# Polynomial work of a fused convolution and attention kernel in two units of three rounds instead of three of two

## The chip, the core and the metric

The kernel runs on one core of a Trainium2 chip. The metric is the time of one execution on the device in microseconds (us), the median of three runs. The traces come from one further execution, taken by the hardware profiler.

## What is computed

The input `x` is 32 images of 64 channels and 56 x 56 positions. Two layers follow each other. Cut to what matters:

```
# layer 0: in each of 8 groups of 8 channels, all products of two and of three channels
p2 = x[:, :, I2] * x[:, :, J2]                    # 36 products
p3 = x[:, :, I3] * x[:, :, J3] * x[:, :, K3]      # 120 products
l  = x + (p2 . W2 + b2) * beta2 + 0.1 * (p3 . W3 + b3) * beta3
# layer 1: for each image, over its N = 56 * 56 = 3136 positions
g   = clip(bn1(conv1x1(l, w_inside)), 0, 6)
f   = theta^T theta                               # theta: the first 32 channels of l
f   = softmax(softmax(f, axis=1), axis=2)
out = bn2(depthwise3x3(g . f)) + l
```

The score matrix `f` is 3136 x 3136 for each image; it is made, normalised twice and used in strips and is never stored.

## The kernel before

**Pairs, steps and halves.** Images go in 16 pairs (`NP`), the two images of a pair on partitions 0 to 63 and 64 to 127. A pair takes `IT` = 49 steps: 24 strips of 128 query positions for its first image, one strip that both share (step 24, `kind == 2`), and 24 for its second. Every step makes 128 x 3136 scores. A step has two halves of 1568 scores. Half `h` counts halves from the start of a pair, so step `t` holds halves `2t` and `2t + 1`.

**One step `t`** (the loop at the end, lines 889 to 931) issues, in this order on TensorE: the scores of the first half (`scores(t, 0)`, into the four banks of the tile `ps`), the attention matmuls of the step three earlier (`attend(u, ...)` with `u = t - LAG`, `LAG` = 3) up to block `split(t)`, then whatever was put at `aux0`; then the scores of the second half, the rest of the attention blocks, and whatever was put at `aux1`. VectorE evicts each half of the scores from `ps` into the tile `e`, keeping the minimum of the negated scores (lines 553 to 561). ScalarE makes two passes over `e`: the exponential with its sum (`first_softmax(t)`), and, for the step before, the exponential of the normalised values (`second_softmax(t - 1)`). The tile `ps` has one buffer, `e` has four.

**Attention** is summed over the strips in PSUM: 25 blocks of 2 x 64 positions by 65 columns, 21 of them in the banks `av0` to `av2`, the last four in the first 260 columns (`AUX`) of the bank `ax`. At an image's end `take` (line 605) divides these sums out of PSUM on VectorE: for the second image of a pair parts 0 and 1 after step 2 of the next pair, parts 2 and 3 in its step 3; for the first image in step 27. Step 27 attends the shared strip for both images.

**The other columns of `ax`** (252) serve two kinds of small work, one after another, called units:

- *Polynomial units.* The layer 0 output of the next pair is made in 13 chunks (`NPC`) of 242 positions. A chunk has six rounds; in a round four matmuls (one for each image and half of its channels) add products of channels to `ax`. The products are made by GpSimd (`products`, line 362; 4 of the first round, `q`, then 4 in each of four rounds and one in the last, `p`) from copies of `x` that SP loads (`prefetch`). GpSimd may be ahead by 8 `q` and 20 `p` tiles (`ROOM`). After the sixth round VectorE adds bias and `x` and writes `y` (`poly_out`, line 469).
- *g units.* The 1 x 1 convolution of three strips (`g_in`, six small matmuls; the ninth unit of an image has one), and its clipping into `gq` by VectorE (`g_out`).

Between units VectorE refills the columns of `ax` with zeros or with the bias (`prepare`, line 443).

**The schedule of the units** is written out for each pair `n` (lines 803 to 854). Each unit gets a half; an even half means `aux0`, an odd one `aux1`, so always behind that half's attention matmuls. For pairs 1 to 14 the three units of a chunk, with two rounds each, go to successive even halves; `BETWEEN` says how many g units follow after which chunk (first the current pair's second image, then the next pair's first), and they take the next free halves. Pair 0 and pair 15 have rules of their own. `split` (line 702) chooses how many attention blocks come before the second half's scores: a unit weighs `1 + 3.6 * rounds` blocks, a g unit 4, and the blocks are shared so that the two halves of a step weigh the same, between 7 and 17.

**Depthwise convolution.** 45 taps a pair on VectorE (`conv_step`) are spread over halves in which no unit ends (`leaves`, line 874).

**Order.** Every instruction is pinned behind the one before it on its engine (`pin`, line 89), so the order of issue above is the order of execution. Line 108 is the helper through which all instructions pass, and so the profile's rows all say L108: they are told apart by tile.

Of the kernel before, what the change touches and what calls it, by code (L numbers as in the profile page):

```python
# [24 lines left out]
NQ = N // QT  # L25
# [44 lines left out]
def tile_poly_conv_attention(  # L70
# [362 lines left out]
    def feed(n, c, ks):  # L433
        todo = [("x0" if name == "0" else "xs", name, k) for k in ks for name in "0a"]
        for name in "24bc":
            todo += [("xc", name, None)] if name == "c" else [("xs", name, k) for k in ks]
        for tag, name, k in todo:
            plan.append((tag, (n, c, ks, name, k)))
        feeds.append((products(n, c, ks), None))
# [78 lines left out]
    def tile_at(t):  # L518
        n, r = divmod(t, IT)
        return n, (0 if r < NQ else 2 if r == NQ else 1), r % (NQ + 1)  # L520
# [103 lines left out]
    def turn(b, h):  # L624

        if h == 0:
            tr = rp.tile([128, 2, NBL * QR], FP, name=f"tr_{b}", tag="tr")
            nums[b] = nums[b], tr
        num, tr = nums[b]
        dve.transpose(tr[:, h, :], num[:, h, :, :].rearrange("p i c -> p (i c)"))  # L630

    def place(b, h):

        _, tr = nums[b]
        o0 = (b % 2) * C + h * 32
        for j in range(2):
            blocks = N // QB - NBL if j else NBL
            for r in range(2):
                k = 2 * j + r
                dst = tt[o0 : o0 + 32, j * NBL * QB : (j * NBL + blocks) * QB]  # L640
                start(
                    dst.rearrange("p (i r q) -> p i r q", r=2, q=QR)[:, :, r, :],
                    tr[k * 32 : k * 32 + 32, h, : blocks * QR].rearrange("p (i q) -> p i q", q=QR),
                )
        if h == 1:
            del nums[b]
# [32 lines left out]
    def put(t, at, what):  # L679
        beside.setdefault((t, at), []).append(what)  # L680
# [5 lines left out]
    LAG = 3  # L686
    ALL, ONE, TWO = (0, 1, 2, 3), (0, 1), (2, 3)
# [32 lines left out]
    def poly_unit(n, c, ks, rs, hs):  # L720
        ends = rs[-1] == NRND
        unit(
            hs,
            FOR_POLY,
            lambda: poly(n, c, ks, rs),
            (lambda: poly_out(n, c, ks)) if ends else None,
            1 + 3.6 * len(rs),
        )
        if ends and c == NPC - 1:
            for j in (0, 1):  # L730
                if 2 * j in ks:

                    t = hs // 2 + 1 if j == 0 or n == 0 else (n * IT) + 2
                    put(t, "loads", lambda j=j: load_theta(2 * n + j))

    def g_unit(n, qs, j, hs):
        unit(hs, FOR_G, lambda: g_in(n, qs, j), lambda: g_out(n, qs, j), 4)
# [3 lines left out]
    def ready(qs):  # L741

        end = min(N, (qs[-1] + 1) * QT)
        return next(c for c, (p, w) in enumerate(PCS) if p + w >= end)
# [55 lines left out]

    BETWEEN = {0: 1, 1: 3, 2: 1, 3: 3, 4: 1}, {7: 1, 8: 1, 9: 1, 10: 3, 11: 1, 12: 2}
    for n in range(NP):
        base = n * IT
        gb = [("g", n, qs, 1) for qs in GS]
        ga = [("g", n + 1, qs, 0) for qs in GS]

        def rounds(m, c, ks, per):
            return [("p", m, c, ks, list(range(r, r + per))) for r in range(0, NRND + 1, per)]  # L810

        todo = []
        if n == 0:
            for c in range(NPC):
                todo += rounds(0, c, TWO, 3)
            todo += gb
            for c in range(NPC):
                todo += rounds(1, c, ALL, 2)
                if c >= NPC // 2 + 1:
                    k = min(2 if c < NPC - 1 else len(ga), sum(ready(g[2]) <= c for g in ga))  # L820
                    todo += ga[:k]
                    ga = ga[k:]
            free = [h for h in range(2, 2 * IT - 5) if h // 2 != NQ + LAG]
            at = [2 * base + free[i * (len(free) - 1) // (len(todo) - 1)] for i in range(len(todo))]
        elif n + 1 == NP:
            todo = gb
            at = [2 * (base + LAG) + 3 + 4 * i for i in range(len(gb))]
        else:
            at = []
            h = 2  # L830
            for c in range(NPC):
                for what in rounds(n + 1, c, ALL, 2):
                    h += h % 2
                    while h in (2 * LAG, 2 * (NQ + LAG)):
                        h += 2
                    todo.append(what)
                    at.append(2 * base + h)
                    h += 1
                for of, between in zip((gb, ga), BETWEEN):
                    for _ in range(between.get(c, 0)):  # L840
                        assert of is gb or ready(of[0][2]) <= c
                        while h in (2 * LAG, 2 * (NQ + LAG), 2 * (NQ + LAG) + 1):
                            h += 1
                        todo.append(of.pop(0))
                        at.append(2 * base + h)
                        h += 1
            assert not gb and not ga and h <= 2 * IT
        for what, hs in zip(todo, at):
            if what[0] == "p":
                poly_unit(*what[1:], hs)  # L850
            else:
                assert what[3] == 1 and hs >= 2 * (base + LAG) or hs > 2 * (base + NQ + LAG) + 1
                assert what[3] == 0 or hs < 2 * (base + NQ + LAG)
                g_unit(*what[1:], hs)
        if n + 1 < NP:
            put(
                max(base - 8, 1), "feed",
                lambda n=n: [feed(n + 1, c, ALL) for c in range(NPC)],
            )
        for b, end in ((2 * n, base + NQ), (2 * n + 1, base + IT - 1)):  # L860
            t = end + LAG
            for h in range(2):
                leaves.add(2 * (t + 2 + h))
                put(t + 2 + h, "gap0", lambda b=b, h=h: turn(b, h))

                put(t + 3 + h if b % 2 else base + IT + h, "loads", lambda b=b, h=h: place(b, h))
# [22 lines left out]
    while t < last + LAG or beside:  # L889
# [3 lines left out]
        if old:  # L893
            n, kind, q = tile_at(u)
# [111 lines left out]
```

## Time and profile before

| | |
|---|---|
| median of three runs | 4962.83 us (4959.59 to 4973.32) |
| the profiled execution's own time | 4963.24 us |
| its span, first to last instruction | 4961.4 us |
| mean granted TensorE clock | 0.988 |
| ScalarE, first exponential `e<-e,nm` | 784 of 2913 ns mean |
| ScalarE, second exponential `e<-e,rz` | 784 of 2896 ns mean |
| VectorE, eviction of a first half `e<-ps` | 784 of 1790 ns mean |
| VectorE, eviction of a second half `e<-ps,nm` | 784 of 1847 ns mean |
| GpSimd, products `p<-q,x`, `p<-q,xb`, `q<-x,xa` | 786, 740 and 732 ns mean |

A row of a timeline gives the start and the duration of an instruction, or of a run of like instructions, in us; then engine, line, operation, destination and source tiles, shape and number; in brackets how long the engine was idle before it and what it waited for. Each matmul of the program appears as two records (`x16` for the eight score matmuls of a half). Matmuls are pipelined, and the end of one is modelled: the distance between starts says more than the durations. A row of waits gives who waited for whom, the total in us, the number of waits and the longest.

### The profile page before, as it was taken

How to read it: one execution, taken by the hardware profiler on the slowest of the kernel's cores; microseconds unless marked ns; L12 is line 12 of the kernel's file. 1: busy time of each engine (PE TensorE's matmuls, PEld its weight loads, DVE VectorE, ACT ScalarE, POOL GpSimd, SP SyncE). 2: the span in 40 equal slices, each digit the busy share in tenths (PEclk: the TensorE clock that was granted, in tenths of full speed). 3: DMA queues.
4: the chain of work that ended last, by engine and by line, in shares of the span. 5: the costliest groups of instructions: out<-in, count | busy, mean ns of one | idle time of the engine just before them, and what ended most of it. 6: DMA issues, size and time to landing. Idle time of an engine off the chain costs nothing.

```text
span 4961.4 us, 263901 instructions
## 1 busy us (share of the span) xinstructions
PE 4711.5 (95%) x118068; PEld 3211.9 (65%) x118068; DVE 4136.2 (83%) x6106; ACT 4554.6 (92%) x2356; POOL 3212.2 (65%) x4325
## 2 busy tenths in 40 slices
PE   6988999999999999999999999999999999999885
PEld 2555666666666666666666666666666666666663
DVE  6545898988888898898988888888888888888787
ACT  1767999999999999999999999999999999999995
POOL 2676685857758586785857678585876858587000
PEclk9999999999999999999999999999999999999997
DMA  7555656565565556556565555656555565654101
GB/s 203 148 154 150 147 143 154 144 149 143 146 148 147 139 150 149 139 143 150 146 146 148 147 142 144 145 152 145 144 150 144 145 145 146 153 142 117 39 8 33
DMA packets 884029, 685.64 MB, mean 138 GB/s; under 512 B 290892, under 2 KB 868428, under 8 KB 878796
## 3 DMA queue, kind: packets, MB, share of 16 engines
q1 hardware_dynamic: 874892, 659.46, 52.1%
q8 instruction: 923, 15.12, 1.3%
q10 hardware_dynamic: 8000, 9.30, 0.6%
q14 instruction: 214, 1.75, 0.1%
HBM read 565.65 MB, written 25.69 MB: 119 GB/s over the span
## 4 chain that ended last, share of the span: by engine, by line
PE 76%; DVE 12%; DMA 3%; issue 3%; ACT 3%; POOL 1%; SPq 1%; ACTq 0%; POOLq 0%; DVEq 0%
PE av L108 33%; PE ps L108 25%; PE ax L108 18%; DVE e L108 10%; ACT e L108 3%; DMA xc_None<-in_x_dram 2%; DVE y L108 1%; SPq L108 1%; POOL p L108 1%; DVE num L108 1%; DMA x<-in_x_dram 1%; DMA first<-in_x_dram 1%; POOL q L108 0%; DMA xa<-in_x_dram 0%; ACTq L108 0%
## 5 line engine op out<-in xcount | busy, mean ns | idle before, releaser
L108 PEld LDWEIGHTS av<-gq,e 128*64 128x64 f32 x64512 | 2015.8, 138 | 945.6 <-issue 938.6
L108 ACT ACTIVATE e<-e,nm 128x3136 f32<-128x3136 f32 x784 | 2283.6, 2913 | 279.9 <-DVE e L108 264.0
L108 POOL TENSOR_TENSOR p<-q,x 128x242 f32<-128x242 f32 (+1 forms) x2418 | 1820.2, 786 | 842.6 <-PE ax L108 834.8
L108 ACT ACTIVATE e<-e,rz 128x3136 f32<-128x3136 f32 x784 | 2270.5, 2896 | 0.0
L108 PE MATMUL av<-gq,e 128*64 128x65 f32 x64512 | 2229.3, 225 | 4.3 <-ACT e L108 3.0
L108 DVE TENSOR_SCALAR_CACHE_REDUCE e<-ps 128x1568 f32<-128x1568 f32 x784 | 1403.4, 1790 | 312.7 <-PE ps L108 295.4
L108 DVE TENSOR_SCALAR_CACHE_REDUCE e<-ps,nm 128x1568 f32<-128x1568 f32 x784 | 1448.3, 1847 | 256.9 <-PE ps L108 251.4
L108 PE MATMUL ps<-th 32*64 32x392 f32 x25088 | 1450.2, 515 | 120.6 <-DVE e L108 110.8
L108 DVE SCALAR_TENSOR_TENSOR y<-tt,wdt,y 128x605 f32<-128x605 f32 (+4 forms) x720 | 726.2, 1009 | 6.7 <-DMA tt<-tr 5.2
L108 POOL TENSOR_TENSOR p<-q,xb 128x242 f32<-128x242 f32 x806 | 574.9, 740 | 218.8 <-PE ax L108 208.5
L108 POOL TENSOR_TENSOR q<-x,xa 128x242 f32<-128x242 f32 x806 | 570.9, 732 | 204.9 <-DMA xa<-in_x_dram 195.5
L108 PEld LDWEIGHTS ps<-th 32*64 32x64 f32 x25088 | 369.9, 130 | 463.1 <-DVE e L108 381.6
L108 PE MATMUL ax<-gq,e 128*64 128x65 f32 x12288 | 490.3, 222 | 1.2 <-issue 1.2
L108 PE MATMUL ax<-p,wq 128*32 128x242 f32 (+1 forms) x6448 | 477.8, 374 | 2.4 <-POOL p L108 1.4
L108 PEld LDWEIGHTS ax<-gq,e 128*64 128x64 f32 x12288 | 425.4, 138 | 1.5 <-issue 1.5
L108 PEld LDWEIGHTS ax<-p,wq 128*32 128x32 f32 x6448 | 178.4, 109 | 108.4 <-POOL p L108 15.7
L108 POOL TENSOR_SCALAR y<-y,bias 128x616 f32<-128x616 f32 (+1 forms) x80 | 149.1, 1864 | 149.2 <-PE ax L108 149.2
L108 DVE SCALAR_TENSOR_TENSOR y<-ax,bias,xc_None 128x242 f32<-128x242 f32 (+3 forms) x208 | 97.1, 467 | 120.7 <-PE ax L108 115.1
L108 POOL TENSOR_TENSOR p<-xc_None 128x242 f32<-128x242 f32 (+3 forms) x208 | 127.6, 614 | 105.2 <-DMA xc_None<-in_x_dram 85.3
L108 PE MATMUL ax<-p,w 128*32 128x242 f32 (+1 forms) x1612 | 125.1, 373 | 33.2 <-POOL p L108 33.2
L108 PE MATMUL ax<-wit,y 128*64 128x64 f32 x3136 | 143.8, 223 | 10.2 <-issue 6.1
L108 ACT ACTIVATION_READ_ACCUMULATOR e<-e,nm 128x1 f32 x784 | 145.7, 186 | 0.0
(80 smaller groups left out, 1348.9 us busy)
## 6 DMA issues: line engine op xcount, KB each, us to landing
x<-in_x_dram SPq DMA_DIRECT2D x2232, 121.0 KB
xa<-in_x_dram SPq DMA_DIRECT2D x744, 121.0 KB
xb<-in_x_dram SPq DMA_DIRECT2D x1488, 60.5 KB
th<-y SPq DMA_DIRECT2D x124, 392.0 KB
xc_None<-in_x_dram SPq DMA_DIRECT2D x360, 121.0 KB
x<-in_x_dram SPq DMA_DIRECT2D x186, 116.0 KB
out_dram<-y SPq DMA_DIRECT2D x64, 308.0 KB
tt<-tr SPq DMA_DIRECT2D x128, 100.0 KB
```

The lines of the kernel that those rows point to most:

```text
L108: i = f(*args, **kw)
```

## The change

A chunk's six rounds go into two units of three rounds. The units no longer have to stand in even halves. Unit `i` of chunk `c` is put at the first free half from `2 + (2c + i) * 10 // 3` on, so that units are 3.33 halves apart where nothing pushes them further; the halves `2 * LAG`, `2 * (NQ + LAG)` and the one after it stay closed. The table of g units is changed in its second part: the first g unit of the next pair comes after chunk 8 instead of 7, and chunk 11 is followed by two instead of one. g units are not put before half `2 * LAG`.

```diff
-    BETWEEN = {0: 1, 1: 3, 2: 1, 3: 3, 4: 1}, {7: 1, 8: 1, 9: 1, 10: 3, 11: 1, 12: 2}
+    BETWEEN = {0: 1, 1: 3, 2: 1, 3: 3, 4: 1}, {8: 1, 9: 1, 10: 3, 11: 2, 12: 2}
...
             at = []
+            shut = (2 * LAG, 2 * (NQ + LAG), 2 * (NQ + LAG) + 1)
             h = 2
             for c in range(NPC):
-                for what in rounds(n + 1, c, ALL, 2):
-                    h += h % 2
-                    while h in (2 * LAG, 2 * (NQ + LAG)):
-                        h += 2
+                for i, what in enumerate(rounds(n + 1, c, ALL, 3)):
+                    h = max(h, 2 + (2 * c + i) * 10 // 3)
+                    while h in shut:
+                        h += 1
                     todo.append(what)
                     at.append(2 * base + h)
                     h += 1
                 for of, between in zip((gb, ga), BETWEEN):
                     for _ in range(between.get(c, 0)):
                         assert of is gb or ready(of[0][2]) <= c
-                        while h in (2 * LAG, 2 * (NQ + LAG), 2 * (NQ + LAG) + 1):
+                        h = max(h, 2 * LAG)
+                        while h in shut:
                             h += 1
```

Pairs 1 to 14 run this code. In it `rounds(m, c, ks, per)` cuts a chunk's rounds into units of `per`.

## The prediction

> **What bounds the kernel now.** I read the page's first part, then the waits over the whole span, then the timeline of TensorE, half step by half step.
>
> ```profile
> PE 4711.5 (95%) x118068; PEld 3211.9 (65%) x118068; DVE 4136.2 (83%) x6106; ACT 4554.6 (92%) x2356; POOL 3212.2 (65%) x4325
> ```
> ```profile
> DVE e L108 <- PE ps L108: 546.8, 929, 8.1
> PEld ps L108 <- DVE e L108: 381.6, 886, 3.2
> ```
>
> TensorE and VectorE wait for each other about 900 times each: a ring. The score tile `ps` has one buffer, so the matmuls of a half fill it, VectorE evicts it into `e`, and only then may the next half's scores start. The timeline of TensorE shows the ring alone where a step has no unit:
>
> ```profile
> 2241.95 0.92 PE L108 MATMUL ps<-th 32*64 32x392 f32 x16
> ...
> 2244.82 0.92 PE L108 MATMUL ps<-th 32*64 32x392 f32 x16 [0.41 <-DVE e L108]
> ...
> 2247.76 1.30 PE L108 MATMUL ps<-th 32*64 32x392 f32 x16 [0.35 <-DVE e L108]
> ```
>
> From scores to scores it takes 2.87 and 2.94 us, with TensorE waiting 0.41 and 0.35 us inside: 5.81 us a step, of which the evictions are 1.79 and 1.85 us (means of the two group rows). ScalarE's two exponentials (2913 and 2896 ns) are 5.81 us too. So no step can be under 5.81 us, and a half can be longer only. Step 7 of the same pair carries a polynomial unit of two rounds and a g unit:
>
> ```profile
> 2008.00 0.92 PE L108 MATMUL ps<-th 32*64 32x392 f32 x16
> ...
> 2010.16 0.62 PE L108 MATMUL ax<-p,wq 128*32 128x242 f32 x8
> 2010.60 0.59 PE L108 MATMUL ax<-p,w 128*32 128x242 f32 x8
> 2011.12 0.91 PE L108 MATMUL ps<-th 32*64 32x392 f32 x16
> ...
> 2014.21 0.92 PE L108 MATMUL ps<-th 32*64 32x392 f32 x16
> ```
>
> Here the halves are 3.12 and 3.09 us, together 6.21, and TensorE has no wait: its own work sets them. The next step is 5.81 us again (2014.21 to 2020.02). What a long step lost, no later one wins back. So **the time is the sum over halves of the greater of the ring and TensorE's work**, and work that fits under the ring is free.
>
> **TensorE's work in a half**, from the spacing of starts in that timeline: scores 0.84 us; attention 0.13 plus 0.119 per block (8 blocks 1.08, 13 blocks 1.67); the last four blocks in `ax` 0.47; a unit of two rounds 0.96; a full g unit 0.34. A step without units is then 2.40 + 2.51 = 4.91, hidden under 5.81. With a two-round unit `split` moves blocks (8 and 17), and it is 2.88 + 2.98 = 5.86, as the timeline has it at 2020.02 to 2025.88: the unit costs 0.05 of its 0.96. A g unit in the same step adds 0.35 in full.
>
> **The period before** (49 steps, one pair): 28 steps with a two-round unit at 5.86 = 164.1; 10 with unit and g unit at 6.21 = 62.1; one with unit and the single-block g unit, 6.05; 8 without a polynomial unit at 5.81 = 46.5 (two g units in one step also fit); step 27 (the shared tile) 7.83; step 3 (evacuating the other accumulator) 6.69. Sum 293.2. The timeline has pair 5 from 1672.21 to 1965.75: 293.5.
>
> **The third round.** Period 0 has three-round units for two images in its timeline:
>
> ```profile
> 120.64 0.60 PE L108 MATMUL ax<-q,wq 128*32 128x242 f32 x4
> 121.07 1.03 PE L108 MATMUL ax<-p,wq 128*32 128x242 f32 x8
> 122.03 0.91 PE L108 MATMUL ps<-th 32*64 32x392 f32 x16
> ```
>
> 1.39 us from first round to scores; another (132.37 to 133.71) 1.34. In step 7 a round follows a round after 0.44, so 0.96 + 0.44 = 1.40. I take 0.44 more than a two-round unit (bounds 0.38, from 1.34, and 0.52, the last round's distance to the scores).
>
> **The change, placed by its own arithmetic.** Units fall at halves 2, 5, 8, 12, 16, 18, 22, 25 and so on: 26 different steps of the 49. Seven also hold a g unit in their odd half (steps 6, 9, 29, 36, 39 after an even unit; 14 before an odd one; 16 the single block). `split` gives 7 and 18 blocks round an even unit (3.19 + 3.11), 17 and 8 round an odd one (2.99 + 3.31): 6.30 either way, over the ring in both halves. That is 0.49 above 5.81, where two two-round units paid 0.05 each. Per period: 19 steps at 6.30 = 119.7; 6 with a full g unit at 6.21 + 0.44 = 6.65: 39.9; one with the single block 5.98 + 0.44 = 6.42; 21 steps without polynomial unit at 5.81 = 122.0; step 27 still 7.83.
>
> **Step 3 gets dearer.** Chunk 0's second unit now ends in the odd half of step 2, just where VectorE evacuates the accumulator banks:
>
> ```profile
> 1983.18 0.18 DVE L108 RECIPROCAL rd<-av 128x7 f32<-128x7 f32 x1
> ...
> 1984.17 0.62 DVE L108 TENSOR_TENSOR num<-av,rd 128x448 f32<-128x448 f32 x1
> 1984.71 1.78 DVE L108 TENSOR_SCALAR_CACHE_REDUCE e<-ps 128x1568 f32<-128x1568 f32 x1
> ```
>
> This takes 1.53 us and starts as soon as the eviction ends; the scores of step 3 wait behind it. In the changed order of VectorE, `y<-ax` and the copy into `ax` stand ahead of it, and `y` needs the last polynomial matmul. What they take after a unit is seen in step 7 (scores start 2011.12):
>
> ```profile
> 2011.26 0.47 DVE L108 SCALAR_TENSOR_TENSOR y<-ax,bias,xc_None 128x242 f32<-128x242 f32 x1 [0.44 <-PE ax L108]
> 2011.76 0.36 DVE L108 COPY ax<-bias1r 128x192 f32<-128x192 f32 x1
> 2012.14 1.85 DVE L108 TENSOR_SCALAR_CACHE_REDUCE e<-ps,nm 128x1568 f32<-128x1568 f32 x1
> ```
>
> So the evacuation starts 1.0 us after the scores and the eviction 2.53 after them, not 1.43: +1.10, step 3 = 7.79 (bounds 0 and 1.5). The g unit of step 3 lies under its slow second half (3.42).
>
> **Edits at nothing.** VectorE's output and refill per chunk are as many as before; elsewhere they fit between scores and eviction, as the three rows above do (the eviction still begins 1.02 us after the scores). Conv taps move into halves without units, with less cover; the longest (1.3 us) could push an eviction by 0.1 to 0.2, in some three halves: 0 to 0.5 us a period, taken as 0. GpSimd: every product is still issued at least six halves (17 us) ahead of its matmul, and one chunk needs 25 products at about 0.75 us = 19 us in 6.7 halves (20 us), so it keeps up; in the steady stretch before, no wait of TensorE for GpSimd is listed. SP: 26 loads per chunk at 0.6 us = 16 us in the same 20. The theta loads after the last unit (step 42 or 43) have five steps. Pairs 0 and 15 keep their schedule.
>
> **Sum.** After: 119.7 + 39.9 + 6.4 + 122.0 + 7.8 + 7.8 = 303.6; before 293.2; +10.4 a period, in 14 periods +146. The profiled execution took 4963.2 (span 4961.4), so 4963.2 + 146 = **5109 us**; the median of the runs, 4962.8, is the same within 0.4.
>
> **Two rules against the rows.** The trace shows a fixed cost of 0.96 − 2 × 0.44 = 0.08 us per unit. The Trainium skill, "TensorEngine Tiling (Array Packing)", section Key Properties, says a change of tiling mode drains TensorE; a unit of 128x32 tiles between 128x64 and 32x64 ones adds such a change, and the edit saves 13 of them. By the row this is worth 13 × 0.08 = 1.0 us a period and is in the sum. By the roughly 175 ns drain that "TensorE: Matmul & The Clock Gate" (Single matmul latency) gives, it would be 2.3, an estimate, and the sum 5091. The row is taken. Against the change speaks "Perfetto Trace Analysis" (Matmuls): independent groups should rotate through PSUM banks, so that an eviction overlaps the next group. The 0.41 us wait shows that this kernel cannot. With such a rotation TensorE's spare 0.9 us in a light step would pay for heavy ones and only its total would count (285.2 us a period after, against 286.3 before).
>
> **Rivals.**
> - **Slack carries over** (faster). Place: the four `e` buffers and the lag of three steps. If they smooth unequal steps, a period falls to TensorE's 285.2, about 8.3 less than 293.5: 4963 − 116 = 4847. It decides if a step after a long one may be under 5.81. For it: ScalarE is behind VectorE by up to a step. Against: after 6.21 comes 5.81 or 5.86. 3%.
> - **Products come late** (much slower). GpSimd's 19 of 20 us leave little; if each second unit waited 1 us, 13 us a period, +182: about 5290. For it: its queue waited 81 us on loads in the steady stretch. Against: six halves of lead. 8%.
> - **The extra work is mostly hidden** (no change, within the 0.3% or 15 us that runs of this kernel can tell apart): needs a three-round unit at about 1.0 us; both rows above say 1.34 or more. 2%.
> - The forecast: 87%.
>
> **How the numbers follow.** Bounds: third round 0.38 or 0.52 in 26 units and 14 periods, −22 or +29; step 3, −15 or +6; taps, up to +7. 5109 − 37 = 5072 and 5109 + 42 = 5151; these ends hold the forecast, and with its 87% cover eight in ten. Slower: forecast and late products, 95%; same 2%; faster 3%.
>
> **What would show it.** In the changed profile: steps with a unit at about 6.30, steps without at 5.81; 1.40 us from a unit's first matmul to the scores; step 3's first eviction 2.5 us after its scores; ScalarE's idle time on VectorE up by about 145 us; TensorE's busy share lower. It is wrong if unit-free steps fall under 5.8, if heavy steps stay below 6.1, or if TensorE waits for `p` in the steady stretch.

## The result, and the profile after

| | before | after |
|---|---|---|
| median of the runs | 4963.57 us (4959.59 to 4973.32) | 5103.3 us (5097.03 to 5105.91) |
| the profiled execution | 4963.24 us | 5101.96 us |
| granted TensorE clock | 0.988 | 0.990 |
| a pair (2 to 14), scores to scores | 293.4 to 294.5 us | 302.9 to 304.6 us |

The changed kernel is slower: ratio 1.0276 (95% interval 1.0261 to 1.0291). The forecast was 5109 us.

The first part of the page of after, busy time by engine:

```profile
PE 4713.6 (92%) x118068; PEld 3228.9 (63%) x118068; DVE 4119.4 (81%) x6106; ACT 4554.3 (89%) x2356; POOL 3175.0 (62%) x4325
```

Every engine has the work that it had within 1.2% (TensorE 4711.5 us before, ScalarE 4554.6) and the same number of instructions; only the span grew. The clock is no cause: from 600 us to the end of pair 14 the granted TensorE clock is 1.00 in both traces. So the 139 us are waiting, and the waits of after over the whole span say where (who waited for whom: total in us, number, longest):

```profile
DVE e L108 <- PE ps L108: 675.0, 1078, 8.2
ACT e L108 <- DVE e L108: 418.3, 636, 23.5
PEld ps L108 <- DVE e L108: 415.8, 871, 3.2
PE ps L108 <- DVE e L108: 237.2, 597, 2.0
```

VectorE waits 128 us more for scores (546.8 before), ScalarE 154 us more for VectorE (264.0 before). TensorE waits for the eviction more too, 34 us by the row that was shown before (381.6) and 126 us by the row `PE ps`, which was 110.8: it has long halves and idle ones side by side. The chain of work that ended last has shifted in the same way (shares of the span by engine; TensorE had 76% and VectorE 12% before):

```profile
PE 63%; DVE 24%; issue 6%; DMA 3%; ACT 3%; POOL 1%; SPq 1%; ACTq 0%; POOLq 0%; DVEq 0%
```

More of the chain now runs through an eviction, because more halves are set by the ring. The start of pair 6 on TensorE's timeline in after has a light step, two steps with a unit and step 3 in a row (a bracket of 0.35 or 0.41 on a row of scores says that the half before it was light):

```profile
2018.11 0.92 PE L108 MATMUL ps<-th 32*64 32x392 f32 x16 [0.35 <-DVE e L108]
2020.98 0.92 PE L108 MATMUL ps<-th 32*64 32x392 f32 x16 [0.41 <-DVE e L108]
2023.92 0.92 PE L108 MATMUL ps<-th 32*64 32x392 f32 x16 [0.35 <-DVE e L108]
2024.77 1.04 PE L108 MATMUL av<-gq,e 128*64 128x65 f32 x28
2025.74 0.62 PE L108 MATMUL ax<-q,wq 128*32 128x242 f32 x8
2026.17 1.01 PE L108 MATMUL ax<-p,wq 128*32 128x242 f32 x16
2027.11 0.91 PE L108 MATMUL ps<-th 32*64 32x392 f32 x16
...
2030.20 0.91 PE L108 MATMUL ps<-th 32*64 32x392 f32 x16
...
2033.18 0.91 PE L108 MATMUL ps<-th 32*64 32x392 f32 x16
...
2036.47 0.91 PE L108 MATMUL ps<-th 32*64 32x392 f32 x16
2038.38 1.85 PE L108 MATMUL av<-gq,e 128*64 128x65 f32 x56 [1.00 <-DVE rd L108]
2040.77 0.92 PE L108 MATMUL ps<-th 32*64 32x392 f32 x16 [0.53 <-DVE e L108]
2044.19 0.92 PE L108 MATMUL ps<-th 32*64 32x392 f32 x16 [0.65 <-DVE e L108]
```

Step 0 has no unit: 2018.11 to 2023.92 is 5.81 us. Step 1 has one behind its first half: 3.19 + 3.09 = 6.28. Step 2 has one behind its second: 2.98 + 3.29 = 6.27. Neither has a wait of TensorE. The unit takes 2025.74 to 2027.11, that is 1.37 us, to the next scores. Step 3 is 4.30 + 3.42 = 7.72, where it was 6.69. The rows of VectorE in the same place:

```profile
2036.61 0.47 DVE L108 SCALAR_TENSOR_TENSOR y<-ax,bias,xc_None 128x242 f32<-128x242 f32 x1 [0.47 <-PE ax L108]
2037.11 0.36 DVE L108 COPY ax<-bias1r 128x192 f32<-128x192 f32 x1
2037.38 0.20 DVE L108 RECIPROCAL rd<-av 128x7 f32<-128x7 f32 x1
...
2038.92 1.78 DVE L108 TENSOR_SCALAR_CACHE_REDUCE e<-ps 128x1568 f32<-128x1568 f32 x1
```

The division of the accumulator, from `rd` on, starts only after `y` and the refill of `ax`, and the eviction comes 2.45 us after the scores of 2036.47.

**The account.** The median of each step over pairs 2 to 13 of after gives 17 unit steps at 6.27, two with chunk 12 at 6.22, six with a g unit at 6.62, the one with the single-block g unit at 6.39, 20 light steps at 5.81 and one at 5.87, step 27 at 7.84 and step 3 at 7.72: 302.87 us a pair. Pairs of before are 293.4 where nothing disturbs them: +9.47, in 14 pairs +133. The remaining 6 are the excess of single pairs over these medians (pair 1: 312.7 against 300.8; four long taps, of which more below). The 139 us are thereby placed; what causes them was tried as follows.

### The profile page after: what moved, and what is told of

Same layout as the page of the kernel before. It is cut to its first block, busy times and chain, and to the rows that moved or that the text cites. A ratio compares the mean times of both kernels' runs of the same rounds, so it can differ in the third digit from the quotient of the medians.

```text
span 5100.2 us, 263817 instructions
## 1 busy us (share of the span) xinstructions
PE 4713.6 (92%) x118068; PEld 3228.9 (63%) x118068; DVE 4119.4 (81%) x6106; ACT 4554.3 (89%) x2356; POOL 3175.0 (62%) x4325
## 4 chain that ended last, share of the span: by engine, by line
PE 63%; DVE 24%; issue 6%; DMA 3%; ACT 3%; POOL 1%; SPq 1%; ACTq 0%; POOLq 0%; DVEq 0%
PE ps L108 25%; PE av L108 22%; DVE e L108 20%; PE ax L108 15%; ACT e L108 3%; DVE y L108 2%; DMA xc_None<-in_x_dram 1%; POOL p L108 1%; DVE num L108 1%; DMA x<-in_x_dram 1%; SPq L108 1%; PE first_s L108 0%; DVE ax L108 0%; DMA first<-in_x_dram 0%; DMA xa<-in_x_dram 0%
## 5 line engine op out<-in xcount | busy, mean ns | idle before, releaser
L108 ACT ACTIVATE e<-e,nm 128x3136 f32<-128x3136 f32 x784 | 2283.1, 2912 | 421.8 <-DVE e L108 418.3
L108 PEld LDWEIGHTS av<-gq,e 128*64 128x64 f32 x64512 | 2013.0, 138 | 958.1 <-issue 940.8
L108 POOL TENSOR_TENSOR p<-q,x 128x242 f32<-128x242 f32 (+1 forms) x2418 | 1777.0, 768 | 874.3 <-PE ax L108 867.1
L108 ACT ACTIVATE e<-e,rz 128x3136 f32<-128x3136 f32 x784 | 2270.4, 2896 | 0.0
L108 PE MATMUL av<-gq,e 128*64 128x65 f32 x64512 | 2225.8, 225 | 17.1 <-DVE rd L108 14.0
L108 DVE TENSOR_SCALAR_CACHE_REDUCE e<-ps,nm 128x1568 f32<-128x1568 f32 x784 | 1448.6, 1848 | 349.0 <-PE ps L108 342.5
L108 PE MATMUL ps<-th 32*64 32x392 f32 x25088 | 1453.2, 515 | 248.5 <-DVE e L108 237.2
L108 DVE TENSOR_SCALAR_CACHE_REDUCE e<-ps 128x1568 f32<-128x1568 f32 x784 | 1403.6, 1790 | 343.4 <-PE ps L108 332.5
L108 POOL TENSOR_TENSOR q<-x,xa 128x242 f32<-128x242 f32 x806 | 577.8, 739 | 327.5 <-DMA xa<-in_x_dram 313.3
L108 PEld LDWEIGHTS ps<-th 32*64 32x64 f32 x25088 | 371.1, 130 | 556.2 <-DVE e L108 415.8
L108 DVE SCALAR_TENSOR_TENSOR y<-tt,wdt,y 128x605 f32<-128x605 f32 (+4 forms) x720 | 709.5, 986 | 6.7 <-DMA tt<-tr 5.2
L108 POOL TENSOR_TENSOR p<-q,xb 128x242 f32<-128x242 f32 x806 | 548.9, 710 | 149.4 <-DMA xb<-in_x_dram 143.0
L108 PE MATMUL ax<-gq,e 128*64 128x65 f32 x12288 | 490.3, 222 | 0.0
L108 PE MATMUL ax<-p,wq 128*32 128x242 f32 (+1 forms) x6448 | 445.2, 371 | 1.9 <-POOL p L108 0.5
L108 PEld LDWEIGHTS ax<-gq,e 128*64 128x64 f32 x12288 | 425.1, 138 | 0.0
L108 PEld LDWEIGHTS ax<-p,wq 128*32 128x32 f32 x6448 | 197.5, 109 | 126.7 <-POOL p L108 20.2
L108 POOL TENSOR_SCALAR y<-y,bias 128x616 f32<-128x616 f32 (+1 forms) x80 | 170.9, 2137 | 157.1 <-PE ax L108 157.1
L108 POOL TENSOR_TENSOR p<-xc_None 128x242 f32<-128x242 f32 (+3 forms) x208 | 131.2, 631 | 189.9 <-DMA xc_None<-in_x_dram 163.3
L108 DVE SCALAR_TENSOR_TENSOR y<-ax,bias,xc_None 128x242 f32<-128x242 f32 (+3 forms) x208 | 97.0, 466 | 155.6 <-PE ax L108 142.1
L108 PE MATMUL ax<-p,w 128*32 128x242 f32 (+1 forms) x1612 | 123.9, 370 | 33.2 <-POOL p L108 33.2
L108 PE MATMUL ax<-wit,y 128*64 128x64 f32 x3136 | 143.5, 223 | 10.2 <-issue 6.0
L108 ACT ACTIVATION_READ_ACCUMULATOR e<-e,nm 128x1 f32 x784 | 145.6, 186 | 0.0
```

The source lines that it names most:

```text
L108: i = f(*args, **kw)
```

## The experiments

**The theory of size**: the time is the sum over halves of the greater of ring and TensorE's work, so a unit of three rounds costs 0.46 us in a step wherever it stands (6.27 against 5.81), and step 3 its own 1 us. Rivals: **the placing**, units in odd halves cost (VectorE's work behind them, the division in step 3); **any work**, more work on TensorE costs in every half, and the light ones are not free; **the taps**, pushed into other halves, cost. All runs were timed beside the kernel before, at 4961 to 4962 us on their chip.

**1. Units of three rounds in even halves only.** The size is kept, the placing undone:

```diff
                 for i, what in enumerate(rounds(n + 1, c, ALL, 3)):
                     h = max(h, 2 + (2 * c + i) * 10 // 3)
+                    h += h % 2
                     while h in shut:
-                        h += 1
+                        h += 2
```

> The changed kernel with its three-round units on even halves only. Theory (a half lasts as long as the longer of the score ring and TensorE's own work; the size of the unit is the cost): 16 steps with a unit at 6.27, 9 with unit and full g unit at 6.62, one at 6.39, 21 light steps at 5.81, step 3 back at 6.69, step 27 at 7.84: 302.8 us a pair, as the changed kernel's 302.9; so 5103 us, within 8. Rival (the odd halves are the cost, since VectorE's output and refill then stand ahead of the next step's first eviction): most of the 138 us goes away, under 5010.

Measured: 5158.8 us (5154 to 5182), ratio 1.0407 (1.0382 to 1.0431). The medians of the steps are as the theory of size has them, 302.94 us a pair, and step 3 fell to 6.73. But in 11 places one tap of the depthwise convolution lasts about 8 us. VectorE's timeline there:

```profile
2190.23 0.08 DVE L108 DVE_READ_ACCUMULATOR e<-ps 128x1 f32 x1
2190.23 7.97 DVE L108 SCALAR_TENSOR_TENSOR y<-tt,wdt,y 128x605 f32<-128x605 f32 x1
2198.12 1.84 DVE L108 TENSOR_SCALAR_CACHE_REDUCE e<-ps,nm 128x1568 f32<-128x1568 f32 x1
...
2203.46 0.84 DVE L108 SCALAR_TENSOR_TENSOR y<-tt,wdt,y 128x605 f32<-128x605 f32 x1
```

GpSimd's timeline in the same stretch:

```profile
2187.59 2.72 POOL L108 TENSOR_TENSOR q<-x,xa 128x242 f32<-128x242 f32 x4
2190.26 7.29 POOL L108 TENSOR_TENSOR p<-q,x 128x242 f32<-128x242 f32 x11
2209.53 0.72 POOL L108 TENSOR_TENSOR p<-q,x 128x242 f32<-128x242 f32 x1 [11.98 <-PE ax L108]
```

A tap of the same shape takes 0.84 us a few microseconds later, with no product beside it. The long one starts with a run of 11 products and ends 0.65 us after the run's last (2197.55): it was kept out by all eleven. The next eviction waits behind it, and with it the ring. TensorE's timeline, and below it a stretch before the stall and one at its end (length; busy time of PE, PEld, DVE, ACT and POOL, with the number of instructions; then the granted TensorE clock, the share of DMA, GB/s):

```profile
2200.02 1.61 PE L108 MATMUL ps<-th 32*64 32x392 f32 x16 [6.21 <-DVE e L108]
2201.56 2.60 PE L108 MATMUL av<-gq,e 128*64 128x65 f32 x48
2204.09 0.91 PE L108 MATMUL ps<-th 32*64 32x392 f32 x16
```
```profile
2186.00:2192.00 6.00, 6.00 (x154) 3.95 (x150) 4.82 (x6) 5.69 (x4) 6.00 (x10) 1.00 0.58 175
2197.00:2203.00 6.00, 2.98 (x42) 1.77 (x44) 5.06 (x6) 3.00 (x3) 0.55 (x1) 0.50 0.53 137
```

TensorE stands still for 6.21 us, and the stall costs more than that: the granted clock is 0.50 from 2197 to 2203 us, and the scores behind the wait take 1.54 us to the next matmuls instead of 0.84. In all 11 places the half that waits is 6.1 to 6.6 us over its median, and the half after it, part of it at the lower clock, 0.9 to 1.5 us. In the profiled execution (5182 us) eleven such stalls of about 7 us are the 80 us over 5102. So the steps speak for size and against placing, and the total for the taps, in a form that no theory had listed. Whether even units cost as much as odd ones in the total could be said only once the long taps were gone (7 below).

**2. No unit behind the second half of step 2.** Takes the unit of step 2 away from the division, `shut = (5, 2 * LAG, ...)`.

> The changed kernel with half 5 closed too, so that the second unit of chunk 0 moves from the odd half of step 2 to the odd half of step 3, where VectorE's evacuation already makes the half 3.42 us. Theory: step 3 falls from 7.72 to 6.69 and hides the unit (TensorE's work there is 3.28), step 2 becomes light, but g units shift into steps with units: 301.7 us a pair against 302.9, 14 pairs, 17 us less: 5086. Rival (the unit in step 3 is not hidden): 301.7 + 0.5, 5093 or more. If the evacuation delayed nothing: 5103 or more.

Measured: 5097.0 us (5094.9 to 5099.5), ratio 1.0273 (1.0257 to 1.0288): 6 us under the median of after where 17 were expected. By the medians of its steps it gains nothing (303.0 us a pair); it has one long tap where after has four. Step 2 is light now, and step 3 hides the unit in its second half (3.29), but its first half is 4.68, not 3.27; step 3 is 7.97. With a unit in the odd half `split` puts 17 blocks of attention before the second scores, and the last three of them are in the third bank of the accumulator, which VectorE divides out only after the first eviction. The first half of step 3 on TensorE's timeline of this run (`x12` are the last three blocks):

```profile
2032.90 0.92 PE L108 MATMUL ps<-th 32*64 32x392 f32 x16 [0.35 <-DVE e L108]
2033.83 1.85 PE L108 MATMUL av<-gq,e 128*64 128x65 f32 x56
2037.08 0.57 PE L108 MATMUL av<-gq,e 128*64 128x65 f32 x12 [1.40 <-DVE rd L108]
2037.58 0.91 PE L108 MATMUL ps<-th 32*64 32x392 f32 x16
```

(The row with `[1.00 <-DVE rd L108]` above is a wait of the same kind in after, for the first bank.) The expectation had left that wait out.

**3 and 4. The same work under the ring and over it.** A dummy g unit (six small matmuls with zero weights into the columns of `ax` that a g unit uses, 0.34 us more in a half) goes 12 times into each of pairs 1 to 14: in 3 behind the first halves of light steps, in 4 behind the second halves of steps with an even unit, which are full. The sums are unchanged, since zeros are added.

```diff
+    for n in range(1, NP - 1):
+        for t in (5, 10, 15, 18, 20, 23, 25, 30, 35, 44, 45, 46):
+            put(n * IT + t, "aux0", idle_unit)
```

In 4 the list is (1, 4, 8, 11, 19, 21, 24, 26, 28, 31, 34, 38) and the place `"aux1"`.

> The changed kernel with the work of one g unit more (six 64-column matmuls with zero weights into the free columns of ax, 0.34 us of TensorE) in the first half of 12 steps without units, in each of pairs 1 to 14. Theory: TensorE's work in those halves goes from 2.40 to 2.74, under the ring's 2.88: no cost, 5103 within 6. Rival (TensorE's total counts, slack is shared between steps): 12 x 14 x 0.34 = 57 us more, 5160, the same as in x4_heavy. Second rival (slack is shared and ScalarE sets the time): neither costs anything.

> The same extra work of 0.34 us, but in the second half of 12 steps that have a three-round unit in their first half. Theory: those halves go from 3.09 to 3.43, all of it is paid: 12 x 14 x 0.34 = 57 us more, 5160 within 8. Rivals: the same as x3_light, both +57 if TensorE's total counts, both 0 if ScalarE sets the time.

Measured: 5095.7 us in light halves (5094.96 to 5098.16; ratio 1.0271, 1.0254 to 1.0288) and 5155.5 in full ones (5146.8 to 5156.7; ratio 1.0387, 1.0371 to 1.0402). A light half that holds it, on TensorE's timeline of 3:

```profile
1898.88 0.91 PE L108 MATMUL ps<-th 32*64 32x392 f32 x16
1899.72 1.62 PE L108 MATMUL av<-gq,e 128*64 128x65 f32 x48
1901.17 0.52 PE L108 MATMUL ax<-zz 128*64 128x64 f32 x12
1901.75 0.92 PE L108 MATMUL ps<-th 32*64 32x392 f32 x16
```

2.87 us from scores to scores, as without it. A full half on the timeline of 4:

```profile
1907.50 0.91 PE L108 MATMUL ps<-th 32*64 32x392 f32 x16
1908.35 1.85 PE L108 MATMUL av<-gq,e 128*64 128x65 f32 x56
1910.03 0.64 PE L108 MATMUL ax<-gq,e 128*64 128x65 f32 x16
1910.49 0.52 PE L108 MATMUL ax<-zz 128*64 128x64 f32 x12
1910.94 0.91 PE L108 MATMUL ps<-th 32*64 32x392 f32 x16
```

3.44 us where it was 3.09. The same instructions cost nothing in one place and 60 us in the other; a pair grows from 302.84 to 306.98, by 12 times 0.345. This is the rule of the forecast, and the rival of any work falls. Run 3 lies 7.6 us under after, just outside its range; the pairs it changes have the same length (302.84 and 302.87), and pair 0, whose schedule is untouched, was 4.9 us shorter in its trace (399.2 against 404.1). Two things the runs do not separate. ScalarE's two exponentials take 5.81 us a step, as the ring does, so it is not shown that a shorter ring alone would shorten a light step. And `split` loads the two halves of a step about alike, so whether slack could pass between the halves of one step was not tried; that it does not pass between steps is what the two runs show.

**5. Step 3 with the blocks shared otherwise.** Run 2, and in step 3 no more than 14 blocks in its first half:

```diff
-        return min(max(round((NBL - d) / 2), PER), 2 * PER + 3)
+        return min(max(round((NBL - d) / 2), PER), 2 * PER + (0 if t % IT == LAG else 3))
```

> x2_late with at most 14 attention blocks ahead of the second half's scores in step 3. In x2_late the first half of step 3 is 4.68 us, not 3.27. Theory: split put 17 blocks there to make room for the unit, and the last three need the third accumulator bank, which VectorE evacuates only after the first eviction of that step. With 14 blocks the first half is 3.3 us and the second 3.64: 6.95 instead of 7.97 in step 3, 14 us less than x2_late: 5083, within 6. Rival (VectorE's output behind the unit is what delays it): no change, 5097.

Measured: 5089.6 us (5088.7 to 5092.2), ratio 1.026 (1.0243 to 1.0277). Step 3 is 3.31 + 3.71 = 7.02, against 7.97 in run 2 and 7.72 in after. The reading of the wait in run 2 holds, and of after's loss what step 3 can give back is 14 us by the medians, 10 by its length (0.70 in 14 pairs). The total fell only 7 us under run 2, half of what was expected; by its length step 3 gives 13 (0.95 in 14 pairs), and this run has three taps of 2.3 to 2.8 us where run 2 has one.

**6. Taps moved off the places where they starved.** Run 1 has its stalls in steps 24 and 34. First the halves 49 and 69 are closed to taps, then in a second kernel 48 and 68 instead, since the stalls left in step 34 came from a tap issued in the half before:

```diff
+    leaves |= {2 * n * IT + h for n in range(1, NP - 1) for h in (49, 69)}
```

> The changed kernel on even halves (x1_even) with no conv tap in halves 49 and 69 of pairs 1 to 14. In x1_even the taps there last 7.8 to 8.3 us instead of 0.8 in 11 places, each until a run of 11 or 12 GpSimd products ends. Theory (the tap starts as that run starts and is kept out by it): without a tap there, no stall; every step at its own length, 302.9 us a pair and 5100 us, within 10. Rival (the even halves themselves cost it, or the next tap meets the same run): 5140 or more.

> x5_even_taps with the closed halves one earlier, 48 and 68: a tap put at half 68 runs between the evictions of step 34's two halves and so lengthens the half that the trace lists as 34, second; x5 closed 49 and 69 and missed it (three stalls of 6.1 us stayed in step 34). Theory: no tap meets the start of the long GpSimd run, no stall, 303 us a pair, 5103 us, within 10. Rival (any tap near that run stalls, wherever it is put): 5120 or more.

Measured: 5125.5 us (5118 to 5130.6; 1.0329, 1.0314 to 1.0345), with the stalls of step 24 gone and three of 6.1 us left in step 34; and 5161.6 us (5146 to 5169; 1.0401, 1.0377 to 1.0425), with 14 taps of 4.1 to 4.6 us in other steps, step 35 above all. The first lies between its two expectations, the second on the side of its rival. Closing halves moved the stall: two halves were not to blame, and taps starve elsewhere when a long run of products meets them there.

**7. A short break between products.** Run 1, and after every second product GpSimd clears a tile of one column:

```diff
+            if k % 2:
+                pool.memset(brk, 0.0)
```

> The changed kernel on even halves (x1_even), and GpSimd clears a 128 x 1 tile after every second product. In x1, x5, x8 and x9 every tap of over 1.6 us started while GpSimd multiplied and, but for three, ended 0.60 to 0.71 us after the last product of an unbroken run. Theory (GpSimd's next product keeps the tap out [...]; an instruction of GpSimd that reads nothing lets it in): no tap over 2 us, every step at its own length, 303 us a pair, 5103 us, within 12. Rival (the stalls have another cause, or the small instructions cost GpSimd too much): taps of 4 to 8 us stay, 5140 or more.

Measured: 5097.6 us (5095.5 to 5098.6), ratio 1.0275 (1.026 to 1.0291), against 5158.8 without the break. No tap is longer than 2.12 us. GpSimd's groups show what it paid:

```profile
L108 POOL MEMSET brk<- 128x1 f32 x2015 | 203.8, 101 | 0.0
```

204 us more of work on GpSimd took 61 us off the time. It also settles the placing: units of three rounds in even halves alone cost what after costs within 6 us (5103.3), and a step with a unit is 6.27 us in both, behind an even half or an odd one. So it is their size and not the odd halves. That the totals agree is in part a balance: step 3 gives back 0.99 us, and nine steps instead of six hold a unit and a full g unit, which takes about 1.0 again.

**8. The other way round: two-round units, g units in light steps.** If the rule holds, the kernel before can be made faster by taking the g units out of steps with a unit. The schedule of before is written as a table: units of two rounds in even halves, g units two to a step in steps 7, 11, 15, 19, 30 and 46 to 48, one in 3 and one in 45.

```diff
+            steps = [t for t in range(IT) if t not in (3, 7, 11, 15, 19, NQ + LAG, 30, 46, 47, 48)]
+            gs = [(2 * LAG + 1, 1, 0)] + [(2 * t + k, 1, 0) for t in (7, 11, 15, 19) for k in (0, 1)]
...
+            polys = [w for c in range(NPC) for w in rounds(n + 1, c, ALL, 2)]
+            for t, what in zip(steps, polys):
+                plan_.append((2 * t, what))
```

> The kernel before (two-round units on even halves), with a written table: the 39 units in 39 steps, 17 of the 18 g units in the eight steps that hold no unit and in the odd half of step 3, one in the odd half of step 45. Theory: in the kernel before ten steps with unit and full g unit cost 0.35 each and one 0.19; now one does; the turn of step 30 meets two g units, up to 0.7 more: a pair 290 to 290.6 instead of 293.4, 14 pairs, 39 to 48 us less: 4919, within 8. Rival (g units are not free in light steps, since each adds 0.7 us of VectorE): 4963 or more.

Measured: 5035.0 us (5033 to 5048), ratio 1.0154 (1.0139 to 1.0169): slower, where 4919 was expected. The number is on the rival's side, but not for the rival's reason: steps 7, 11 and 46 to 48, with two g units each, are 5.81 us. Most steps have the length that the rule gives. Two things had been left out. The last chunk now ends in step 45, and the loads of `th` for the next pair come late; the first half of step 0 is 7.68 us, and in 10 of pairs 2 to 14 the granted clock falls to 0.50 there, as behind the stalls of run 1. The waits of this kernel:

```profile
PEld ps L108 <- DMA th<-y: 43.2, 31, 3.3
```

Before had 7.0 us there. The other part is longer halves in step 8 (the second up to 5 us longer; in pair 10 a tap waits there 2.58 us for GpSimd, whose `q` products had waited for loads of `xa`) and in steps 29 and 30 (6.2 to 6.3 us a step). A second table ends the last chunk in step 44, has no g units in step 30 and no taps in halves 16 and 17:

> x7_lightg with the last chunk ending in step 44 again instead of 45, and no tap before step 9. In x7_lightg every step had the length of the theory except step 0, 7.7 us in its first half instead of 2.88, waiting for the theta loads, and step 8, whose second half waited up to 5 us. Theory: with the theta loads issued at step 45 as in the kernel before, both waits go: 38 steps at 5.86, one at 6.21, eight light ones with g units at 5.81, 7.84 and 6.69: 289.9 us a pair, 14 pairs x 3.5 = 49 us less than the kernel before: 4914, within 8. Rival (25 steps of units in a row outrun GpSimd's products, or the loads are late again): 4963 or more.

Measured: 5024.2 us (5022 to 5048), ratio 1.0137 (1.0113 to 1.016). With the last chunk a step earlier the first half of step 0 is 2.89 us again. Its undisturbed pairs are 291.2 to 291.6 us, 2 less than before, but 12 taps of 4.6 to 7.9 us eat it up. So last the break of run 7 was added to it:

> x9_lightg2 with the same small clears on GpSimd. In x9 the pairs without a long tap took 291.2 to 291.6 us and those with one or two 296 to 306. Theory: no long tap, 291.5 us in every pair, 14 pairs x 2.0 less than the kernel before: 4935, within 12. Rival (GpSimd, with ten small instructions a chunk more, falls behind 25 steps of units in a row): 4963 or more, with TensorE waiting for p.

Measured: 4945.6 us (4934 to 4968), ratio 0.9971 (0.9961 to 0.9982): within its expectation, and faster than the kernel before by 0.3%; the interval leaves out 1, but the difference is small, and the two ranges overlap (4957 to 4968 us for the kernel before). Most pairs are 290.5 to 292.2 us. The kernel before was not run with the break alone; it has no tap over 1.5 us for a break to shorten. Two long taps remained, of 5.38 and 8.19 us, across 8 and 12 products with breaks between: the break makes the stall rare and does not exclude it.

## Why the prediction was right, step by step

- **The rule of the sum over halves: shown.** The trace has light steps at 5.81 behind steps of 6.27 in every pair, and runs 3 and 4 charge the same instructions 0 and 60 us.
- **The third round: 0.44 forecast, 0.41 measured** (1.37 from unit to scores against 0.96). Unit steps are 6.27 and not 6.30, those with a g unit 6.62 and not 6.65. In 26 units and 14 pairs this is 11 us, and it is the term that put the forecast above the result. The value lies between the two rows that the prediction had: 0.44 between two rounds of one unit, and 0.38 from the unit of 1.34. The two lengths of a unit also bear on the two rules that it weighed: 0.96 and 1.37 us give 0.41 a round and leave 0.14 as the fixed cost of a unit (an estimate from these two, good to a few hundredths), between the 0.08 of its row and the 0.175 of the other rule. What part of the 0.14 is the change of tiling no run isolates.
- **Step 3: +1.10 forecast, +1.03 measured.** The order (`y` and the refill ahead of the division) is as foreseen, with the eviction 2.45 us after the scores instead of 2.53. That TensorE itself waits there for a divided bank (1.00 us) was not in the working; it lies beside the wait for the eviction, since the next scores still wait 0.53 us for that, and so cost nothing in after, but it decided run 2.
- **The count of steps: right**, 19, 6, 1 and 21 by kind, and step 27 the same.
- **Edits at nothing: right in the sum, wrong in one reason.** GpSimd has 21 products a chunk, not 25, so some 16 us in 20. TensorE has no new wait for `p` in the steady stretch. Taps were given 0 to 0.5 us a pair; four of 2.8 us in after cost 1.1 to 1.4 each, 5 in all. That is within the bound, but the cause was not the cover of a half: a tap can be kept out by a whole run of products, and the forecast had taken one tap of 1.3 us for the worst. Runs 1 and 7 show that it can be 61 us with the same units in other halves (5158.8 us, and 5097.6 with the break); that the changed kernel escapes it was not foreseen, and is luck.
- **The rivals.** Slack carrying over would need steps under 5.81: none is. Products late would show as waits for `p`: none are new. A mostly hidden third round would need steps under 6.1: none with a unit is.
- **What would show it.** ScalarE's idle time on VectorE rose by 154 us, foreseen 145; TensorE's busy share fell from 95% to 92%.

The sum again by measured terms: 9.47 a pair where 10.4 was forecast, 133 in 14 pairs, and 6 from single pairs, 139 in all for 146. The 6 were not in the forecast; without them its error would have been 13 us instead of 7.

## What to carry to other kernels

Where two engines pass one buffer back and forth, work is added up half by half: find for each half whether the ring or the engine's own work is longer, and put small work into the halves where the ring is. Merging small units into fewer and larger ones can be a loss even when it saves fixed costs: here a step hid all but 0.05 us of a unit of 0.96, and 0.46 of one of 1.37 stood out. And before a schedule is moved, look for instructions with two SBUF inputs on VectorE beside long unbroken runs on GpSimd: a stall of 6 us cost 7 here, since the granted clock of TensorE was halved behind it.

## What was not expected of the hardware

A tap reads two tiles in SBUF on VectorE; a product reads SBUF on GpSimd. The Trainium skill, "SBUF — State Buffer", section "Who interferes with whom", says that such a pair contends for a shared read port, an exclusive lock that is held for a whole instruction, and that an instruction that only writes does not contend. In most cases the runs agree: a tap takes 0.84 us with no product beside it or near the end of one, and about 1.3 when it starts with one of 0.7 us, so it waits for the rest of one product; some that start in the last 0.1 us of a product take about 1.4, as if they waited for the next one too. By that rule the worst tap would be about 1.6 us, an estimate from 0.84 and 0.79, the longest of the three product means shown. The measurement decides against it: of the 9360 taps in all 13 traces 96 lasted over 1.6 us and 77 over 1.8, up to 8.28. All but three of the 96 waited to the end of a run of products, broken by nothing but the short clears of runs 7 and 8, and ended 0.59 to 0.71 us after its last product. In after the longest is 2.85 us across 4 products; in before none is over 1.5. Clears that only write, set between the products, brought the longest down from 8.28 to 2.12 us in the same schedule (run 7) and left two of 5.38 and 8.19 us in another (run 8). Which tap is let in after one product and which is kept out to the end stays open: where in a product the tap starts does not decide it alone, and no run isolates it.
